# Four graph layers on one core: the opening reordered, idle TensorE slots filled, and the two arms of a branch exchanged

## The chip, the cores and the metric

The kernel runs on one core of a Trainium2 chip. The metric is the device time of the program in microseconds; three runs of the kernel before gave 1700.79, 1702.48 and 1705.91, median 1702.48. The core has a matrix engine (TensorE, PE in the profile, with its weight loads listed as PEld), a vector engine (VectorE, DVE), an activation engine (ScalarE, ACT), a general engine (GpSimd, POOL) and a queue engine (SyncE, SP) that issues every data transfer here. Each engine takes its own list of instructions in order and waits on semaphores where it needs another's result.

## The reference, cut to what matters

32 graphs of 512 nodes with 128 features share one adjacency matrix of 512 by 512 zeros and ones. Each of four layers adds its result for `relu(layernorm(x))` to `x`:

```
x = x + gnn0(h)      # x_h = elu(h @ Wi + bi); e = sigmoid(a_tgt[i] + a_src[j] + be) * mask[i, j]
                     # recv = elu([e @ x_h, x_h * sum_j e] @ Wn + bn); out = [recv, x_h] @ Wm + bm
x = x + gnn1(h)      # 5 steps of a gated unit on m = adj @ h:
                     #   z, r = sigmoid(...); hv = tanh(m @ w5 + (r * h) @ u5); h = (1 - z) h + z hv
x = x + gnn2(h)      # adj @ (h @ weight) + bias
x = x + gnn3(h)      # sum over powers 0 to 3 of adj, each with a weight
```

`mask` is `adj`, with 0.005 in place of its zeros.

## The kernel before

A graph is a 128 x 512 tile, and most operations work on one such tile: TensorE products in float32 against a 128 x 128 weight, copies and activations on ScalarE, additions on VectorE. Graphs are loaded in groups of four; the last layer works on a whole group.

**The order is written out beforehand.** The kernel lists operations with an engine, an assumed duration and a due time, and the class `Plan` sorts them into one order by list scheduling: at each moment of its own clock each engine takes the ready operation that is due first, provided that its buffers are free (36 of kind `f`, 8 PSUM banks of kind `b`, and so on). The order of the instructions of each engine is therefore fixed when the kernel is built; on the chip only semaphores move them. The due time of graph b starts at `begin(b)` (L627): 10 planner microseconds per graph for the first ones (`FIRST_PACE`), 56 per graph in the steady part, 30 at the end.

**Two arms.** Products with the adjacency can take a cheap path with a rounded float32 format (`float32r`), in which one operand is split into a high and a low part, if the adjacency is exactly representable in it. The kernel tests this on the chip: the adjacency is transposed on TensorE (L464), copied as `A_r` in the rounded format by ScalarE (L466), compared with the original on VectorE (L472, with a count per partition), and TensorE sums the counts (L479) into `inexact` (L484). The operations whose planned start lies before `BRANCH`, 30 planner microseconds, are issued first; then every engine loads `inexact` (L906) and branches (L907). Behind it stand two complete orders of all the rest, `arm(False)` for any adjacency, written first, and `arm(True)` for an exact one, written second and reached by a jump. The adjacency of this case is exact.

**What precedes the branch.** SP issues the loads in the order graph 0, `Wi`, the four adjacency blocks `A_nat`, `bi`, the token weights `W_tok`, `be`, graph 1, `Wn` and the others, graphs 2 and 3. Each graph's `layernorm` (L425) takes statistics on DVE (L434 to L437), an inverse square root on POOL (L439) and scaling on ACT (L447). `layer0` (L503) transposes h on TensorE (L334), copies it (L394), multiplies by `Wi` (L405), applies `elu` (three activations L492, L410, L495, two DVE steps L497, L499), multiplies into tokens and scores (L521), spreads the target scores (L558), forms four masked score tiles (L572 on ACT, L575 on DVE), aggregates with four products (L583), sums rows with four products against `ones` (L590 through L405), and continues with `Wn` (L611) and `Wm` (L619). `mask` comes from two steps for each transposed block (L468, L469).

**After the branch** the arm transposes the gate weights (L674), permutes the adjacency (L757), and runs layers 1 to 3. Layer 1's step has the adjacency product (L769), three gate weights, and the candidate product with `u5T`, which waits for DVE's reset gate times h (L801). Layer 3 is L850 and L859.

Of the kernel before, what the change touches and what calls it, by code (L numbers as in the profile page):

```python
# [10 lines left out]
F32 = mybir.dt.float32  # L11
# [3 lines left out]
ALU = mybir.AluOpType  # L15

P = 128
ALPHA = 0.005
# [20 lines left out]
class Plan:  # L39
# [13 lines left out]
    def op(self, eng, us, due, emit, reads=(), writes=(), two=False, keep=0, result=None):  # L53

        o = Op(eng, us, self.RESULT[eng] if result is None else result, emit, two, keep)
        for v in reads:
            o.before.add(v.writer)  # L60
        for v in writes:
            o.before.update(v.readers)
            if v.writer:
                o.before.add(v.writer)
            elif v.kind and v.slot is None:
                o.takes.append(v)
        for v in reads:
            v.readers.append(o)
# [34 lines left out]
    def order(self, end=None):  # L103
# [82 lines left out]
def tile_four_graph_layers(  # L186
# [79 lines left out]
    ident, ones, neg_half = const("ident", [P, P]), const("ones", [P, P]), const("nhalf", [P, NC])  # L266
    op("POOL", 1.0, -9, lambda: make_identity(nc, at(ident)), [], [ident])
    op("DVE", 0.2, -9, lambda: nc.vector.memset(at(ones), 1.0), [], [ones])
    op("POOL", 0.2, -9, lambda: nc.gpsimd.memset(at(neg_half), -0.5), [], [neg_half])
    ones_r = const("ones_r", [P, P], F32R)  # L270
    op("POOL", 0.4, 5, lambda: nc.gpsimd.tensor_copy(at(ones_r), at(ones)), [ones], [ones_r])
# [3 lines left out]
        at(warm)[:, :1], at(ones)[:, :1], AF.Tanh), [ones], [warm])  # L275


    def load(v, src, due, us=0.5, to=None):
        op("SP", us, due, lambda: nc.sync.dma_start(at(v) if to is None else to(at(v)), src), [], [v])
        return v  # L280

    def load_const(src, shape, name, due, us=0.5):
        return load(const(name, shape), src, due, us)
# [8 lines left out]
    plan.vals.update(dict.fromkeys([*X_group, *X]))  # L292

    def load_graph(b, due):
        op("SP", 1.5, due, lambda: nc.sync.dma_start(
            at(X[b]), x[b].rearrange("(c p) d -> p c d", p=P)),
            [], [X_group[b // G], X[b]] if b % G == 0 else [X[b]])

    load_graph(0, -9)
    Wi_sb = load_const(Wi, [P, P], "Wi_sb", -9)  # L300
    A_nat = [Val("f") for _ in range(NC)]
    for ic in range(NC):
        load(A_nat[ic], adj[ts(ic, P), :], -8, 1.3)
    bi_sb = load_column(bi, "bi_sb", -8)
# [6 lines left out]
    load_graph(1, -6)  # L311
# [145 lines left out]
    A_r, mask = const("A_r", [P, NC, N], F32R), const("mask", [P, NC, N])  # L457
    inexact = const("inexact", [1, 1], I32)
    n_odd = const("n_odd", [P, NC])
    for jc in range(NC):  # L460
        pt, z, odd = Val("b"), Val("f"), Val("f")
        def turn(jc=jc, pt=pt):
            for ic in range(NC):
                nc.tensor.transpose(at(pt)[:, ts(ic, P)], at(A_nat[ic])[:, ts(jc, P)], at(ident))  # L464
# [3 lines left out]
        op("ACT", T_COPY, jc, lambda z=z, pt=pt: nc.scalar.mul(at(z), at(pt), 1 / ALPHA), [pt], [z])  # L468
        op("DVE", T_VEC, jc, lambda jc=jc, z=z, pt=pt: nc.vector.scalar_tensor_tensor(  # L469
            at(mask)[:, jc, :], at(pt), 0.0, at(z), op0=ALU.is_equal, op1=ALU.add),  # L470
            [pt, z], [mask])
# [173 lines left out]
    issue(plan.order(end=BRANCH))  # L645
    assert inexact.writer.begun
    common = plan.state()

    def arm(exact):
        with ExitStack() as stack:  # L650
            pool = stack.enter_context(tc.tile_pool(name=f"arm{exact:d}", bufs=1))
            plan.back_to(common)
            list_rest(exact, pool)
            issue(plan.order())

# [251 lines left out]
    with tc.If(taken > 0) as branch:  # L907
        arm(False)
    with branch.Else():
        arm(True)  # L910


# [33 lines left out]
```

## Time and profile before

| | |
|---|---|
| Three runs, median | 1702.48 us (1700.79 to 1705.91) |
| The profiled execution's own time | 1704.23 us |
| Its span | 1702.4 us |
| Busy in the span: PE, DVE, ACT, POOL | 1665.6, 1478.8, 1099.6, 377.3 us |
| Mean granted TensorE clock | 0.996 |
| Data moved | 156.5 MB, 92 GB/s |

The page gives busy time per engine, the same in 40 equal slices (a digit is the busy share in tenths, PEclk the granted clock in tenths), the chain of work that ended last, and groups of instructions. A line of a timeline reads: start and duration in us, engine, source line, operation, result and operands, number of records, and in brackets the idle time before it with what ended it. A float32 product appears as two records. In answers by stretch, the columns are the stretch, its length and then busy time with the number of instructions for each engine, the granted clock, the share of the transfer engines and GB/s. The names of an engine with a q at the end are its sequencer.

### The profile page before, as it was taken

To read this page: it belongs to the slowest core of one execution; us is meant where nothing else is said; L and a number is where in the kernel's file an instruction comes from. 1 tells how busy PE (TensorE), PEld (TensorE's weight loads), DVE (VectorE), ACT (ScalarE), POOL (GpSimd) and SP (SyncE) were. 2 spreads that over 40 slices of the span, in tenths; PEclk is the share of its full clock that TensorE was granted. 3 is DMA by queue.
4 is the path that set the end of the run, shared out by engine and by line. 5 is a ranking of instruction groups with operands and counts; after the bars stand their busy time and mean duration, and the time that the engine had idled before them with its cause. 6 is when DMAs were issued, how large, how long until landed. Compare 5 with 4: busy or idle time off the path is not lost.

```text
span 1702.4 us, 21136 instructions
## 1 busy us (share of the span) xinstructions
PE 1665.6 (98%) x6521; PEld 1065.7 (63%) x6521; DVE 1478.8 (87%) x3325; ACT 1099.6 (65%) x2075; POOL 377.3 (22%) x301
## 2 busy tenths in 40 slices
PE   5999999999999999999999999999999999999998
PEld 3565555666666666665666665666666666666787
DVE  5789999999989998889989898899999888877842
ACT  5786767777666776566676666667576756655550
POOL 3231122312312222222212222122232221001210
PEclk8999999999999999999999999999999999999999
DMA  3122323253333332242333333333333323222302
GB/s 95 36 69 93 123 96 99 70 150 92 93 99 112 100 105 88 76 123 93 94 108 91 94 107 87 100 107 107 89 112 95 95 86 101 81 75 75 95 6 62
DMA packets 266873, 156.54 MB, mean 92 GB/s; under 512 B 75392, under 2 KB 235008, under 8 KB 266752
## 3 DMA queue, kind: packets, MB, share of 16 engines
q1 hardware_dynamic: 266752, 155.12, 30.9%
q8 instruction: 53, 0.87, 0.2%
q14 instruction: 68, 0.56, 0.1%
HBM read 82.25 MB, written 72.81 MB: 91 GB/s over the span
## 4 chain that ended last, share of the span: by engine, by line
PE 84%; DVE 8%; DMA 3%; ACT 3%; issue 2%; SPq 0%; POOL 0%; DVEq 0%; ACTq 0%; POOLq 0%
PE b L405 39%; PE b L769 18%; PE b L859 9%; PE b L850 6%; PE b L583 4%; PE b L619 3%; DMA f<-d 2%; PE b L521 2%; DVE f L575 2%; PE b L833 1%; DVE r L743 1%; PE b L606 1%; ACT f L447 1%; DVE f L794 1%; DVE f L346 1%
## 5 line engine op out<-in xcount | busy, mean ns | idle before, releaser
L394 ACT COPY f<-b 128x512 f32<-128x512 f32 x360 | 207.8, 585 | 151.6 <-PE b L769 105.8
L769 PE MATMUL b<-AQ,r 128*128 128x512 f32 x1024 | 304.4, 439 | 0.8 <-DVE r L743 0.8
L439 POOL TENSOR_TENSOR s<-s,nhalf 128x4 f32<-128x4 f32 x128 | 156.0, 1219 | 645.8 <-DVE s L437 610.1
L769 PEld LDWEIGHTS b<-AQ,r 128*128 128x128 f32 x1024 | 192.1, 188 | 90.5 <-issue 49.9
L794 DVE TENSOR_TENSOR f<-f,b 128x512 f32<-128x512 f32 x320 | 211.8, 677 | 20.4 <-PE b L405 16.5
L447 ACT ACTIVATE f<-x,s 128x128 f32<-128x128 f32 x512 | 210.1, 488 | 23.0 <-DVE s L442 22.7
L346 DVE STREAM_TRANSPOSE f<-f 128x512 f32<-128x512 f32 x244 | 204.6, 845 | 22.3 <-ACT f L447 21.7
L859 PE MATMUL b<-r,A_r 128*128 128x512 f32 x768 | 223.6, 426 | 0.0
L410 ACT ACTIVATE f<-f,b4w 128x512 f32<-128x512 f32 x160 | 115.4, 723 | 165.2 <-DVE f L794 164.7
L594 POOL TENSOR_TENSOR f<-f,f 128x512 f32<-128x512 f32 x84 | 130.9, 1559 | 307.3 <-DVE f L575 231.0
L405 PE MATMUL b<-f,u5T 128*128 128x512 f32 x320 | 163.9, 596 | 7.9 <-DVE f L801 7.8
L859 PEld LDWEIGHTS b<-r,A_r 128*128 128x128 f32 x768 | 139.0, 189 | 44.9 <-issue 23.0
L405 PE MATMUL b<-f,w4T 128*128 128x512 f32 x320 | 163.4, 593 | 0.2 <-ACT f L394 0.2
L405 PE MATMUL b<-f,u3T 128*128 128x512 f32 x320 | 163.0, 592 | 0.4 <-DMA f<-m 0.4
L405 PE MATMUL b<-f,w5T 128*128 128x512 f32 x320 | 162.8, 592 | 0.0
L405 PE MATMUL b<-f,w3T 128*128 128x512 f32 x320 | 162.5, 592 | 0.0
L769 PE MATMUL b<-A_r,r 128*128 128x512 f32 x512 | 151.8, 439 | 2.5 <-DVE r L743 2.5
L410 ACT ACTIVATE f<-b,b5w 128x512 f32<-128x512 f32 x160 | 109.2, 684 | 64.5 <-PE b L405 63.5
L743 DVE TENSOR_TENSOR r<-f,r 128x512 fp32r<-128x512 f32 x192 | 143.1, 749 | 8.2 <-ACT r L739 8.1
L850 PEld LDWEIGHTS b<-V,f 128*128 128x128 f32 x1024 | 130.5, 192 | 24.8 <-issue 20.6
L410 ACT ACTIVATE f<-f,b3w 128x512 f32<-128x512 f32 x160 | 115.2, 720 | 42.5 <-DVE f L794 41.6
L811 DVE TENSOR_TENSOR f<-f,f 128x512 f32<-128x512 f32 x160 | 114.7, 718 | 29.3 <-ACT f L410 28.7
(103 smaller groups left out, 2623.8 us busy)
## 6 DMA issues: line engine op xcount, KB each, us to landing
m<-f SPq DMA_DIRECT2D x244, 256.0 KB, 2.1
f<-m SPq DMA_DIRECT2D x184, 256.0 KB, 2.9
f<-m SPq DMA_DIRECT2D x240, 64.0 KB, 2.2
x<-in_x_dram SPq DMA_DIRECT2D x32, 256.0 KB, 3.1
out_dram<-x SPq DMA_DIRECT2D x32, 256.0 KB, 2.4
f<-d SPq DMA_DIRECT2D x28, 256.0 KB, 5.1
f<-in_adj_dram SPq DMA_DIRECT2D x4, 256.0 KB, 4.0
f<-in_L_gnn_weight_dram SPq DMA_DIRECT2D x2, 224.0 KB, 3.3
```

The lines of the kernel that those rows point to most:

```text
L346: op("DVE", us, due, lambda: nc.vector.transpose(view_out(at(blocks)), view_in(at(src))), [src], [blocks])
L394: op("ACT", us, due, lambda: nc.scalar.copy(at(t), at(src)), [src], [t])
L405: nc.tensor.matmul(to, at(w), of, start=start, stop=stop)
L410: op("ACT", us, due, lambda: nc.scalar.activation(at(dst), at(src), AF.Tanh, bias=at(bias), scale=scale), [src, bias], [dst])
L439: op("POOL", 1.2, due, lambda: nc.gpsimd.tensor_tensor(stat(SCALE), stat(VAR), at(neg_half), op=ALU.pow), [s, neg_half], [s])
L447: nc.scalar.activation(at(h)[:, ts(c, P)], at(X[b])[:, c, :], AF.Relu, bias=stat(SHIFT)[:, c : c + 1], scale=stat(SCALE)[:, c : c + 1],)
L594: op("POOL", 1.4, d - 10, lambda: nc.gpsimd.tensor_tensor(at(dst), at(a), at(c), op=ALU.add), [a, c], [dst])
L743: op("DVE", T_VEC, due, lambda: nc.vector.tensor_tensor(part(lo), whole(), part(hi).bitcast(F32), op=ALU.subtract), [src, hi], [lo], two=two)
L769: nc.tensor.matmul(at(pa), at(part)[:, ts(jc, P)], view(at(columns)[:, jc, :]), start=jc == n == 0, stop=jc == NC - 1 and n == PARTS - 1,)
L794: op("DVE", T_VEC, d, lambda: nc.vector.tensor_tensor(at(s), at(u), at(pg), op=ALU.add), [u, pg], [s])
L850: nc.tensor.matmul(at(pz)[:, ts(i, D)], at(hT[i])[:, ts(ic, P)], at(V[k]), start=i == 0, stop=last and i == G - 1,)
L859: nc.tensor.matmul(at(pz), at(adjT)[:, jc, ts(ic, P)], at(part), start=False, stop=jc == NC - 1 and n == PARTS - 1,)
```

## The change

- **Loads.** Graph 1 is loaded right behind graph 0, `bi` ahead of the adjacency, graph 2 right behind it, graph 3 ahead of `Wm`; `bm_bc` may not start before the branch.
- **Exactness test.** The test no longer uses the transposed blocks: ACT copies each natural block to a rounded tile `short`, and DVE compares it with the block. The transposes become due at 8, the masks at 9 to 12, and the `A_r` copies at 22.
- **Idle TensorE.** Up to the branch, whenever the planner finds no operation for TensorE, it puts in a 128 x 128 product of `ones` with `ones` into one PSUM bank that is set aside for this and given back at the branch. In the resulting order there are 31 of them at the head, then 1, 1, 15, 1 and 3 between other operations.
- **Planner.** Up to the branch, an engine now leaves a slot empty if an earlier-due operation becomes ready within 0.3 of the duration of the one at hand. Graph loads count 0.65 instead of 1.5, adjacency loads 0.65 instead of 1.3; `FIRST_PACE` is 14 instead of 10; `BRANCH` is 18 instead of 30, so that the branch stands earlier in the list of operations.
- **Arms.** The condition is turned round: `arm(True)` is written first and follows the branch directly; `arm(False)` is reached by the jump. The end of each arm goes to the common end behind both.

```diff
     def op(self, eng, us, due, emit, reads=(), writes=(), two=False, keep=0, result=None,
+           earliest=0.0):
...
+        o.earliest = earliest
...
-            o.ready = max([0.0, *(self.known(b, o) for b in o.before if b.begun)])
+            o.ready = max([o.earliest, *(self.known(b, o) for b in o.before if b.begun)])
...
+                if o is not None and end is not None and any(
+                    c.due < o.due and t < now + 0.3 * o.us for t, _, c in coming[e]
+                ):
+                    heapq.heappush(ready[e], (o.due, index[o], o))
+                    o = None
+                if o is None and e == "PE" and end is not None and self.idle.known <= now:
+                    order.append(self.idle)
+                    self.until[e] = now + self.idle.us
+                    heapq.heappush(events, self.until[e])
...
-    PACE, FIRST_PACE, LAST_PACE = 56.0, 10.0, 30.0
-    BRANCH = 30.0
+    PACE, FIRST_PACE, LAST_PACE = 56.0, 14.0, 30.0
+    BRANCH = 18.0
...
+    spare = places["b"].pop()
+    plan.free["b"].pop()
+    plan.idle = Op("PE", 0.224, 0.0, lambda: nc.tensor.matmul(
+        spare[:, :P], at(ones), at(ones), start=True, stop=True), False, 0)
+    plan.idle.known = 0.4
...
     load_graph(0, -9)
+    load_graph(1, -9)
     Wi_sb = load_const(Wi, [P, P], "Wi_sb", -9)
+    bi_sb = load_column(bi, "bi_sb", -9)
...
-    bm_bc = load_const(bm.partition_broadcast(P), [P, P], "bm_bc", -5)
-    load_graph(2, -4)
-    load_graph(3, -3)
+    bm_bc = load_const(bm.partition_broadcast(P), [P, P], "bm_bc", -5, earliest=BRANCH)
+    load_graph(3, -6)
...
+    for ic in range(NC):
+        short, odd = Val("q"), Val("f")
+        op("ACT", T_COPY, 9, lambda ic=ic, short=short: nc.scalar.copy(
+            at(short), at(A_nat[ic])), [A_nat[ic]], [short])
+        op("DVE", 0.7, 9, lambda ic=ic, short=short, odd=odd: nc.vector.scalar_tensor_tensor(
+            at(odd), at(short).bitcast(F32), 1.0, at(A_nat[ic]),
+            op0=ALU.mult, op1=ALU.not_equal, accum_out=at(n_odd)[:, ic : ic + 1]),
+            [short, A_nat[ic]], [odd, n_odd], two=True)
...
-        op("PE", T_TR, jc, turn, [*A_nat, ident], [pt])
-        op("ACT", T_COPY, jc, lambda jc=jc, pt=pt: nc.scalar.copy(at(A_r)[:, jc, :], at(pt)),
+        op("PE", T_TR, 8, turn, [*A_nat, ident], [pt])
+        op("ACT", T_COPY, 22, lambda jc=jc, pt=pt: nc.scalar.copy(at(A_r)[:, jc, :], at(pt)),
...
-        op("DVE", 0.7, 8, lambda jc=jc, pt=pt, odd=odd: nc.vector.scalar_tensor_tensor(
-            at(odd), at(A_r)[:, jc, :].bitcast(F32), 1.0, at(pt),
-            op0=ALU.mult, op1=ALU.not_equal, accum_out=at(n_odd)[:, jc : jc + 1]),
-            [A_r, pt], [odd, n_odd])
...
-    with tc.If(taken > 0) as branch:
+    with tc.If(taken < 1) as branch:
+        arm(True)
+    with branch.Else():
         arm(False)
-    with branch.Else():
-        arm(True)
```

More of the change, by code (lines that the diff above doesn't have):

```diff
@@ L51, in __init__, with op @@
         self.shared, self.now = 0.0, 0.0
-    def op(self, eng, us, due, emit, reads=(), writes=(), two=False, keep=0, result=None):
+        self.idle = None
+    def op(self, eng, us, due, emit, reads=(), writes=(), two=False, keep=0, result=None,
+           earliest=0.0):
         o = Op(eng, us, self.RESULT[eng] if result is None else result, emit, two, keep)
+        o.earliest = earliest
         for v in reads:
@@ L275, in tile_four_graph_layers, with load, load_const @@
         at(warm)[:, :1], at(ones)[:, :1], AF.Tanh), [ones], [warm])
-    def load(v, src, due, us=0.5, to=None):
-        op("SP", us, due, lambda: nc.sync.dma_start(at(v) if to is None else to(at(v)), src), [], [v])
-        return v
-    def load_const(src, shape, name, due, us=0.5):
-        return load(const(name, shape), src, due, us)
+    def load(v, src, due, us=0.5, to=None, earliest=0.0):
+        op("SP", us, due, lambda: nc.sync.dma_start(at(v) if to is None else to(at(v)), src), [], [v],
+           earliest=earliest)
+        return v
+    def load_const(src, shape, name, due, us=0.5, earliest=0.0):
+        return load(const(name, shape), src, due, us, earliest=earliest)
     def load_column(src, name, due):
@@ L294, in load_graph @@
     def load_graph(b, due):
-        op("SP", 1.5, due, lambda: nc.sync.dma_start(
+        op("SP", 0.65, due, lambda: nc.sync.dma_start(
             at(X[b]), x[b].rearrange("(c p) d -> p c d", p=P)),
@@ L299, in tile_four_graph_layers @@
     load_graph(0, -9)
+    load_graph(1, -9)
     Wi_sb = load_const(Wi, [P, P], "Wi_sb", -9)
+    bi_sb = load_column(bi, "bi_sb", -9)
     A_nat = [Val("f") for _ in range(NC)]
     for ic in range(NC):
-        load(A_nat[ic], adj[ts(ic, P), :], -8, 1.3)
-    bi_sb = load_column(bi, "bi_sb", -8)
+        load(A_nat[ic], adj[ts(ic, P), :], -8, 0.65)
+    load_graph(2, -8)
     W_tok = const("W_tok", [P, P + 2])
@@ L310, in tile_four_graph_layers @@
     be_sb = load_const(be.partition_broadcast(P), [P, 1], "be_sb", -7)
-    load_graph(1, -6)
     Wn_sb = load_const(Wn[P:], [P, P], "Wn_sb", -6)
@@ L459, in tile_four_graph_layers @@
     n_odd = const("n_odd", [P, NC])
+    for ic in range(NC):
[6 more added lines that the diff above has]
+            [short, A_nat[ic]], [odd, n_odd], two=True)
     for jc in range(NC):
-        pt, z, odd = Val("b"), Val("f"), Val("f")
+        pt, z = Val("b"), Val("f")
         def turn(jc=jc, pt=pt):
@@ L464, in turn @@
                 nc.tensor.transpose(at(pt)[:, ts(ic, P)], at(A_nat[ic])[:, ts(jc, P)], at(ident))
-        op("PE", T_TR, jc, turn, [*A_nat, ident], [pt])
-        op("ACT", T_COPY, jc, lambda jc=jc, pt=pt: nc.scalar.copy(at(A_r)[:, jc, :], at(pt)),
+        op("PE", T_TR, 8, turn, [*A_nat, ident], [pt])
+        op("ACT", T_COPY, 22, lambda jc=jc, pt=pt: nc.scalar.copy(at(A_r)[:, jc, :], at(pt)),
            [pt], [A_r])
-        op("ACT", T_COPY, jc, lambda z=z, pt=pt: nc.scalar.mul(at(z), at(pt), 1 / ALPHA), [pt], [z])
-        op("DVE", T_VEC, jc, lambda jc=jc, z=z, pt=pt: nc.vector.scalar_tensor_tensor(
+        op("ACT", T_COPY, 9 + jc, lambda z=z, pt=pt: nc.scalar.mul(at(z), at(pt), 1 / ALPHA), [pt], [z])
+        op("DVE", T_VEC, 9 + jc, lambda jc=jc, z=z, pt=pt: nc.vector.scalar_tensor_tensor(
             at(mask)[:, jc, :], at(pt), 0.0, at(z), op0=ALU.is_equal, op1=ALU.add),
             [pt, z], [mask])
-        op("DVE", 0.7, 8, lambda jc=jc, pt=pt, odd=odd: nc.vector.scalar_tensor_tensor(
-            at(odd), at(A_r)[:, jc, :].bitcast(F32), 1.0, at(pt),
-            op0=ALU.mult, op1=ALU.not_equal, accum_out=at(n_odd)[:, jc : jc + 1]),
-            [A_r, pt], [odd, n_odd])
     p_odd = Val("b")
@@ L647, in tile_four_graph_layers @@
     common = plan.state()
+    places["b"].append(spare)
     def arm(exact):
@@ L652, in arm @@
             plan.back_to(common)
+            plan.free["b"].append((BRANCH, len(places["b"]) - 1))
             list_rest(exact, pool)
```

## The prediction

> **What bounds the kernel now.** I read the page's busy shares and 40 slices first, then busy time by stretch, then TensorE's timeline over the first 45 us, then the chain and the branch line.
>
> ```profile
> span 1702.4 us, 21136 instructions
> PE 1665.6 (98%) x6521; PEld 1065.7 (63%) x6521; DVE 1478.8 (87%) x3325; ACT 1099.6 (65%) x2075; POOL 377.3 (22%) x301
> PE   5999999999999999999999999999999999999998
> PEclk8999999999999999999999999999999999999999
> ```
>
> TensorE is the bound from the second slice on. It is idle 1702.4 - 1665.6 = 36.8 us in all; only there, and where its clock is halved, can a rearrangement gain. The stretches say where (span, PE, PEld, DVE, ACT, POOL, then the clock):
>
> ```profile
> 0.00:10.00 10.00, 3.11 (x12) 2.50 (x13) 1.65 (x11) 4.31 (x9) 2.49 (x12) 1.00 0.69 194
> 10.00:20.00 10.00, 3.14 (x12) 2.06 (x10) 8.71 (x39) 5.47 (x10) 3.82 (x4) 0.80 0.19 55
> 20.00:30.00 10.00, 8.25 (x29) 5.08 (x30) 4.95 (x13) 7.63 (x18) 3.60 (x3) 0.52 0.16 47
> 30.00:40.00 10.00, 7.84 (x28) 4.03 (x27) 3.70 (x15) 5.33 (x12) 2.42 (x4) 1.00 0.43 108
> 40.00:50.00 10.00, 8.95 (x38) 5.25 (x37) 8.46 (x27) 8.99 (x22) 3.99 (x7) 1.00 0.00 0
> 200.00:400.00 200.00, 198.44 (x669) 114.81 (x668) 193.58 (x424) 142.19 (x269) 51.02 (x37) 1.00 0.35 104
> ```
>
> 18.7 us of the idle time lie before 50; from 50 to 200 there is none, from 200 to 1500 some 13.2, after the last matmul 5. DVE at 97% in 200 to 400 is the second bound. TensorE's head:
>
> ```profile
> 6.89 1.63 PE L334 MATMUL b<-ident,f 128*128 128x128 f32 x4 [6.89 <-ACT f L447]
> 8.31 3.62 PE L464 MATMUL b<-ident,f 128*128 128x128 f32 x16
> 11.73 1.42 PE L405 MATMUL b<-f,Wi_sb 128*128 128x512 f32 x2
> 20.61 2.10 PE L521 MATMUL b<-W_tok,f 128*128 128x130 f32 x8 [7.46 <-DVE f L499]
> 26.33 2.08 PE L405 MATMUL b<-f,Wi_sb 128*128 128x512 f32 x2 [1.14 <-ACT f L394]
> 28.20 3.43 PE L583 MATMUL b<-f,f 128*128 128x512 f32 x6
> 31.46 0.60 PE L334 MATMUL b<-ident,f 128*128 128x128 f32 x4
> 34.22 1.12 PE L583 MATMUL b<-f,f 128*128 128x512 f32 x2 [2.16 <-DVE f L499]
> ```
>
> Full-clock prices are in later rows: four transposes 0.44, a 128x512 float32 product 0.86, a token product 0.9 for four, a 128x128 product 0.2225 (1.78 for eight of L619). At these prices the work done before 34.22 is 20 transposes 2.2, Wi twice 1.72, tokens 0.9, count 0.3, spread 0.44, a second and a third graph's transposes 0.88, three of L583 2.58: 9.0 us. So 25.2 us are lost by 34.22, and 1.05 more by 46.2: 26.3. The pieces: 6.9 before the first, 3.2 to 13.15 (slow or paced), 7.5 waiting for graph 0's elu, 2.5 slow, 1.1 idle, 1.7 slow, 2.3 at the branch. The branch's own line, and DVE's idle time behind it:
>
> ```profile
> L907 PEldq COMPARE_BRANCH  x1: 4549/4549/4549, 29.6 to 29.6; - x1
> 32.39 0.69 DVE L497 SCALAR_TENSOR_TENSOR f<-f,f 128x512 f32<-128x512 f32 x1 [4.03 <-issue]
> ```
>
> [...]clock 0.50 from 16 to 29.6, L521 2.10 us there and 1.06 later; the 1.00 shown before 10 does not hold, since sixteen transposes take 3.62 us against 1.76. [...]4.55 us on PE, whose exact arm is the jump's target. [...]the other engines' own records are 45 to 76 ns[...].
>
> **The change part by part.** I walk the new order of each engine with the durations above.
>
> *Loads.* Graph 1 goes ahead of Wi and the adjacency: one 256 KB load, 0.65 us as the adjacency blocks land one after another; plus bi, the four blocks land at about 8.4 instead of 7.5. Hidden, as the fillers end later. Graph 3 passes Wm and the score weights on SP's queue; the score weights, last before the branch, are issued when the last block lands and are there 3.5 later, at 11.9, ahead of the tokens at 17.45. bm_bc moves behind the branch (issued 20.5, landing in 3.9), so POOL's bias additions start near 24.5 instead of 14.8; behind them on POOL wait only gate biases, swap and later norms, and DVE's first addition to x comes after 40. Costs nothing.
>
> *Fillers.* 52 products of ones: 31 from 1.05, then 1, 1, 15, 1, 3 as slots of the fixed order. At 0.445 each while cold; [...]they end at 9.7 to 11.4. I take 10.55. Were they unneeded, transposes could start at 8.4: they cost 2.1 here and buy the clock everywhere after. They take one PSUM bank, given back at the branch; the order found places with seven.
>
> *Graph 0.* Eight adjacency transposes, a filler, h's four: 12.1. ACT copies hT to 12.9, PE does eight more and a filler to 13.2 and Wi to 14.1. ACT's three masks end at 14.65, exp, tanh and relu at 16.55, DVE's second elu step at 17.25; 15 fillers end at 17.45: tokens 17.45 to 18.35, against 20.61 to 22.7.
>
> *Exactness test.* It reads the natural blocks, so four more ACT copies (2.3 us; ACT is 65% busy) while PE runs fillers, and DVE's tests no longer wait for A_r. The count comes at 18.4, inexact at 19.5 instead of 23.5. Two of the A_r copies slip past the branch, ahead of their use at L783 by 8 us.
>
> *Graph 1.* Norm on ACT to 18.8, transposes 19.2, three fillers, spread 20.0 to 20.45, Wi 20.7 to 21.6 (before: 26.33 to 28.2).
>
> *Branch.* The exact arm falls through: a tensor load of 0.5 and a compare of 0.05 in each sequencer, under ACT's score and PE's Wi. Graph 0's first aggregation (28.20 above, in the old order) begins at 22.6: four aggregations 3.44, four row sums 3.44, 0.9 lost waiting for graph 2's norm on ACT, tokens of graph 1, five weight transposes, spread, graph 2's Wi, Wn, four permuting products: 12.3 us of work end at 35.5. Work before the branch is 6.0, so 35.5 - 18.3 = 17.2 us are lost where 26.3 were. After that my walk finds no wait. Gain 9.1.
>
> *The end.* The exact arm now ends with a jump over the other arm. PE's sequencer is at the end at 1693.3 and DVE's at 1697.55, so theirs is hidden. SP issues its last store to 1698.92 and then steps through waits that end at 1701.57, for the store's landing at 1701.45. At SP's 2.7 us from the compare to its first step in the arm it arrives at 1701.6 and needs 0.5 more: +0.7 with the barrier. [...]+2.4 at PE's 4.5. I take 0.7.
>
> *The middle.* Line and wait stay the same:
>
> ```profile
> PE b L405 <- DVE f L801: 7.8, 7, 1.9
> ```
>
> A candidate product (u5) waits for DVE's reset times h. By counts from the new order and the row prices, PE's own work between a w4 product and its u5 product is under 4 us in 16 of 160 places, 23 before. DVE work queued ahead of the 48th adjacency product is about 388 us instead of 394. So no worse; I take 0, with -4 to +5.
>
> Sum: -9.1 + 0.7 + 0 = -8.4: the profiled span goes from 1702.4 to 1694.0 and its own time from 1704.2 to 1695.8. The median of the runs, 1702.5, equals the span, so the forecast is 1694.1.
>
> **The rivals.** *Slower: DVE takes over.* Layers 0 of graphs 4 and 5 are put 16 and 14 planner microseconds later (first pace 14 for 10), toward the stretch where DVE has only 6.4 us spare in 200. One such layer is about 9.8 us of DVE (norm 1.4, four masks 2.5, two elus 2.6, the rest single steps of 0.65 to 0.85), two 19.6. If all of it leaves the 19 us that DVE has free between 50 and 200, PE waits 19.6 - 6.4 = 13 us near 300 to 450: 1707. It decides from 8.4 us. For it: the 97%, and 5.2 us of PE idle between 350 and 500 already. Against: the smaller DVE queue ahead of the 48th product.
>
> *Fillers stay cold.* If none of the 31 is at full clock they end at 14.9, and all after is 4.3 later: 1698.4. For it: TensorE stayed at 0.50 through 4.6 busy us from 20.61.[...]
>
> *The branch doesn't get cheaper.* If falling through costs PE's 4.55 too, the first aggregation is at about 25.7, 3.1 later: 1697.2.[...]
>
> *DVE hides part of the gain* without turning it: 3 to 5 us of new waits, 1697 to 1699.
>
> **How the numbers follow.** Forecast 0.60, with its own range 1690 to 1698; cold fillers 0.07, dear branch 0.06, DVE hiding part 0.11, DVE taking over 0.16. About 0.3% (5.1 us) is what a measurement of this kernel can tell from no change: faster means under 1697.4, slower over 1707.6. The forecast case gives 0.55 faster and 0.05 same; the three middle cases 0.07 and 0.17; the last 0.02 same and 0.14 slower, being centred at 1707 but open upward. Faster 0.62, same 0.24, slower 0.14. The lower end 1689 takes in a middle that loses 4 less; the upper 1704 the middle cases and a part of the last.
>
> **What would show it.** Right: clock 1.00 from about 6 on with no dip, inexact near 19.5, PE's branch record near 0.05, the first aggregation near 22.6, PE idle plus fillers about 17 by 35. SP's last wait some 0.7 us later after its last store. Wrong: PE idle from 200 to 1500 well over 13 us with L801's or L743's successors as its releasers, a second elu step later than 17.5, or fillers that end after 11.5.

## The result, and the profile after

The changed kernel took 1713.45 us (median of 6 runs, 1710.08 to 1715.30) against 1703.74 for the kernel before (6 runs in the same comparison): ratio 1.0056, 95% interval 1.0042 to 1.0070. It is about 10 us slower. The forecast was 1694.1, with a range up to 1704, so the result lies outside it and on the other side.

The page of the changed kernel, in the rows that answer to those of before:

```profile
span 1713.5 us, 21323 instructions
PE 1679.7 (98%) x6625; PEld 1076.3 (63%) x6625; DVE 1480.9 (86%) x3325; ACT 1100.2 (64%) x2079; POOL 379.9 (22%) x301
PE   9999999999999999999999999999999999999998
PEclk9999999999999999999999999999999999999999
```

The first slice is full now, and yet the span is 11.1 us longer. Fillers count as busy here (15.1 us), so a busy share does not show the loss. By stretch (span, PE, PEld, DVE, ACT, POOL, clock, share of the transfer engines, GB/s):

```profile
10.00:20.00 10.00, 10.00 (x91) 9.37 (x90) 7.90 (x29) 8.39 (x19) 1.84 (x3) 1.00 0.09 22
20.00:30.00 10.00, 7.21 (x28) 3.57 (x26) 8.33 (x24) 9.12 (x20) 7.17 (x11) 0.99 0.55 146
30.00:40.00 10.00, 10.00 (x34) 5.88 (x34) 5.26 (x18) 6.38 (x14) 3.04 (x3) 0.84 0.02 6
200.00:400.00 200.00, 195.25 (x672) 113.03 (x671) 195.47 (x421) 142.19 (x268) 49.06 (x35) 1.00 0.36 104
```

TensorE's timeline at the head, changed kernel:

```profile
1.04 9.46 PE L285 MATMUL b<-ones 128*128 128x128 f32 x62 [1.04 <-DVE ones L280]
17.17 1.06 PE L545 MATMUL b<-W_tok,f 128*128 128x130 f32 x8
21.96 2.84 PE L607 MATMUL b<-f,f 128*128 128x512 f32 x6 [0.64 <-DVE f L599]
29.25 0.33 PE L700 MATMUL b<-ident,f 128*128 128x128 f32 x1 [2.15 <-DVE f L698]
31.07 2.91 PE L425 MATMUL b<-f,ones 128*128 128x512 f32 x4
```

Graph 0's tokens start at 17.17 (forecast 17.45), its first aggregation (L607, before L583) at 21.96 (forecast 22.6). Up to there the head came out as walked. The waits between 50 and 1650 did not. TensorE's waits (us in total, times, longest), first two rows of before that stand beside the one shown in the prediction (L801, 7.8 us in 7), then those of the changed kernel (L405, L583, L801, L743 of before are L425, L607, L827, L769 now):

```profile
PE b L769 <- DVE r L743: 3.3, 2, 2.5
PE b L583 <- DVE f L575: 1.0, 1, 1.0
```

```profile
PE b L607 <- DVE f L599: 8.1, 9, 1.8
PE b L425 <- DVE f L827: 8.0, 7, 1.9
PE b L630 <- DVE q L625: 3.0, 4, 1.2
PE b L795 <- DVE r L769: 2.0, 2, 1.2
```

The candidate products wait as before. New are the aggregations of later graphs behind their masked scores (L607), and the row sums (L630): 12.7 us in 12 waits became 22.5 in 26.

**A ledger of lost time.** To compare whole executions I price every TensorE record at full clock from this kernel's own rows: 0.4292 us for a float32 record with 512 columns, 0.2267 for one in float32r, 0.1115 for 128 columns, 0.1095 for a transpose, 0.03 for a record of the count, 0 for a filler. The sum is 1639.1 us in every kernel below. At any moment, the time minus the price of what has begun is what TensorE has lost: waits, slow clock, and small gaps between records. I split it into head (up to 50 us), middle (from 50 to the end of the last product) and end (from there to the end of the span):

```
kernel                                head  middle   end    sum = span - 1639.1
before                                27.1    31.3   4.9    63.3
changed                               20.1    47.5   6.8    74.4
changed, a second execution           20.6    51.9   7.0    79.5
```

The head gained 7.0, the end lost 1.9, and the middle lost 16 to 21 us, which the prediction had put at 0. Each row of this ledger, here and below, is one execution. Executions of the kernel before alone lie between 1700.17 and 1712.14 us, so a difference of a few us between two rows counts only where the ratios below agree with it.

### The profile page after: what moved, and what is told of

Its sections match the earlier page's. It is cut to its first block, busy times and chain, and to the rows that moved or that the text cites. A ratio compares the mean times of both kernels' runs of the same rounds, so it can differ in the third digit from the quotient of the medians.

```text
span 1713.5 us, 21323 instructions
## 1 busy us (share of the span) xinstructions
PE 1679.7 (98%) x6625; PEld 1076.3 (63%) x6625; DVE 1480.9 (86%) x3325; ACT 1100.2 (64%) x2079; POOL 379.9 (22%) x301
## 4 chain that ended last, share of the span: by engine, by line
PE 76%; DVE 14%; DMA 4%; ACT 3%; issue 2%; SPq 0%; DVEq 0%; ACTq 0%
PE b L425 34%; PE b L795 16%; PE b L885 9%; PE b L876 6%; PE b L607 3%; DMA f<-d 3%; PE b L643 3%; DVE f L599 2%; DVE f L366 2%; DVE r L769 1%; PE b L545 1%; DVE f L820 1%; PE b L859 1%; DVE f L841 1%; DVE f L839 1%
## 5 line engine op out<-in xcount | busy, mean ns | idle before, releaser
L795 PE MATMUL b<-AQ,r 128*128 128x512 f32 x1024 | 303.9, 439 | 1.2 <-DVE r L769 0.8
L795 PEld LDWEIGHTS b<-AQ,r 128*128 128x128 f32 x1024 | 192.2, 188 | 92.1 <-issue 48.4
L425 PE MATMUL b<-f,u5T 128*128 128x512 f32 x320 | 164.0, 597 | 8.0 <-DVE f L827 8.0
L885 PEld LDWEIGHTS b<-r,A_r 128*128 128x128 f32 x768 | 139.2, 189 | 47.3 <-issue 25.4
L425 PE MATMUL b<-f,w4T 128*128 128x512 f32 x320 | 163.5, 594 | 0.0
L425 PE MATMUL b<-f,u3T 128*128 128x512 f32 x320 | 162.7, 592 | 0.0
L425 PE MATMUL b<-f,w5T 128*128 128x512 f32 x320 | 162.3, 592 | 0.0
L425 PE MATMUL b<-f,w3T 128*128 128x512 f32 x320 | 161.9, 592 | 0.0
L769 DVE TENSOR_TENSOR r<-f,r 128x512 fp32r<-128x512 f32 x192 | 140.6, 737 | 12.3 <-ACT r L765 12.0
L795 PE MATMUL b<-A_r,r 128*128 128x512 f32 x512 | 150.0, 435 | 1.2 <-DVE r L769 1.2
L430 ACT ACTIVATE f<-f,b3w 128x512 f32<-128x512 f32 x160 | 115.0, 720 | 47.5 <-DVE f L820 45.6
L837 DVE TENSOR_TENSOR f<-f,f 128x512 f32<-128x512 f32 x160 | 108.8, 681 | 29.2 <-ACT f L430 28.8
```

What stands on the lines that cost most here:

```text
L425: nc.tensor.matmul(to, at(w), of, start=start, stop=stop)
L430: op("ACT", us, due, lambda: nc.scalar.activation(at(dst), at(src), AF.Tanh, bias=at(bias), scale=scale), [src, bias], [dst])
L769: op("DVE", T_VEC, due, lambda: nc.vector.tensor_tensor(part(lo), whole(), part(hi).bitcast(F32), op=ALU.subtract), [src, hi], [lo], two=two)
L795: nc.tensor.matmul(at(pa), at(part)[:, ts(jc, P)], view(at(columns)[:, jc, :]), start=jc == n == 0, stop=jc == NC - 1 and n == PARTS - 1,)
L885: nc.tensor.matmul(at(pz), at(adjT)[:, jc, ts(ic, P)], at(part), start=False, stop=jc == NC - 1 and n == PARTS - 1,)
```

## Experiments

The prediction was a gain at the head that reaches the end. Two explanations stood against each other after the result. **Order** (theory A in the expectations): the planner writes the whole rest of the program anew, and the new order is worse. **Taken back** (theory B): TensorE is coupled to DVE, ACT and transfers, so whatever is gained at the head is waited away later. Ratios are to the kernel before in the same comparison, with 95% intervals.

### One part of the change at a time

The kernel before with only the arms exchanged, and the changed kernel with the arms in their old places. Beyond the branch the instructions of each engine stand in the same order as without the edit.

```diff
-    with tc.If(taken > 0) as branch:
-        arm(False)
+    with tc.If(taken < 1) as branch:
+        arm(True)
     with branch.Else():
-        arm(True)
+        arm(False)
```

> The kernel before with nothing changed but the condition and the places of the two arms; every engine's order of instructions in the exact arm stays as it was. Theory A (the re-planned order of the middle is what costs, whatever the head delivers): the head gains [...]some 2 to 3 us by 50 us, the middle keeps its lost time of 31 us between 50 and 1690, the end pays some 1.9 us as in the changed kernel: within 1 us of before. Theory B (DVE and the transfers are a second bound and any head gain is given back in the middle): the middle's lost time grows by the 2 to 3 us: 1.5 to 2.5 us slower than before.

> The changed kernel with the arms in their old places, the exact one reached by the jump; all else, orders included, stays. Theory A: lost time at 50 us grows from 20.1 by 2 to 4, the middle keeps 47, the end gets the 1.9 us back: the changed kernel's time, plus 0 to 2 us. Theory B: the later start is absorbed in the middle, and only the end's 1.9 us show: some 2 us faster than the changed kernel.

Exchanged in the kernel before: 1705.22 us, ratio 0.9999 (0.9988 to 1.0010); head 25.4, middle 31.3, end 6.9. Falling through gains 1.7 at the head, the end pays 2.0, and the middle is 31.3 in both, as theory A had it. So a gain at the head can reach the last product. Put back in the changed kernel: 1708.28, ratio 1.0023 (1.0012 to 1.0034); head 21.0, end 4.9, but a middle of 38.3 instead of 47.5, with the same order of instructions. These two rows exaggerate: the 38.3 is of the fastest of ten executions (1705.14), the 47.5 of the slowest of six (1715.30). By the ratios the kernel with the arms put back is some 5.6 us faster (1.0023 against 1.0056), and neither theory had forecast that.

The end is a jump of SP. Rows of the common end in the changed kernel (operation, count, ns, first and last start):

```profile
L933 SPq COMPARE_BRANCH  x2: 46/48/49, 20.1 to 1708.7; - x2
L933 PEldq COMPARE_BRANCH  x2: 92/1691/3290, 20.6 to 1702.4; - x2
```

```profile
L967 SPq DRAIN  x3: 7/7/13, 1712.7 to 1713.0; - x3
```

SP compares at 1708.7, right behind its last store, and is in its closing drain 4.0 us later; in the trace its first step behind the jump is at 1712.18, 3.4 us after the compare. In the kernel before, SP gets from its last store (issued by 1698.92) to that drain (1701.57) in 2.65 us, the wait for the store's landing included. PE's jump takes 3.29 us too, at 1702.4, but PE's last product ends only at 1706.7.

The changed kernel without fillers (the slots stay in the plan and emit nothing), and with 32 more of them ahead of everything:

```diff
-    plan.idle = Op("PE", 0.224, 0.0, lambda: nc.tensor.matmul(
-        spare[:, :P], at(ones), at(ones), start=True, stop=True), False, 0)
+    plan.idle = Op("PE", 0.224, 0.0, lambda: None, False, 0)
```

```diff
-    issue(plan.order(end=BRANCH))
+    early = plan.order(end=BRANCH)
+    first = early.index(plan.idle)
+    issue(early[:first] + 32 * [plan.idle] + early[first:])
```

> The changed kernel without its 52 products of ones; the planner still reserves their slots, so that every other instruction keeps its place. Shows what the fillers are worth. Theory A: TensorE is at half clock for most of the head, lost time at 50 us rises from 20 to 22 to 26, the middle keeps 47: 2 to 6 us slower than the changed kernel. Theory B: the middle takes up the delay: within 1 us of the changed kernel.

> The changed kernel with 32 more products of ones ahead of its 31, which delays all TensorE work by 32 x 0.2225 = 7.1 us and undoes the head's gain; no other order changes. Theory A: the middle keeps its lost time of 47 us and the whole is 6 to 7 us slower than the changed kernel, near 1720. Theory B: the middle's lost time falls to about 40 and the time stays within 2 us of the changed kernel.

Without: 1709.15, ratio 1.0024 (1.0015 to 1.0033), head 21.0, middle 42.1. With more: 1715.34, ratio 1.0061 (1.0041 to 1.0080), head 24.7, middle 43.0. The fillers are worth only 1 us at the head, and the kernel without them is faster, which neither theory had forecast. A head that is 4.6 us later costs nothing that shows against the changed kernel (1.0061 against 1.0056), as theory B had it. One order of the middle, four heads: 38 to 52 us, and 47.5 and 51.9 with one and the same head. The order alone does not fix the loss, nor does the head.

### The pace, and one transfer that the planner takes for too short

The changed kernel with the old pace of the first graphs, the kernel before with the new one, and the changed kernel once more beside them:

```diff
-    PACE, FIRST_PACE, LAST_PACE = 56.0, 14.0, 30.0
+    PACE, FIRST_PACE, LAST_PACE = 56.0, 10.0, 30.0
```

> The changed kernel with the first pace back at 10 instead of 14. Theory C (the room that the order leaves on TensorE between a graph's token products and its first aggregation sets the middle's loss; it is under 11 us for 6 of the 24 graphs 4 to 27 in the changed kernel, for 2 in the kernel before and for 2 here): the middle loses 33 to 38 us instead of 47, and the time is 1700 to 1706. Theory D (the pace has nothing to do with it, any re-plan behind this head costs as much): 1709 to 1715.

> The kernel before with the first pace at 14 and nothing else. Room under 11 us for 3 graphs of 24. Theory C: the middle loses 31 to 35 us, within 4 us of before. If the first pace itself is to blame: the middle loses 40 or more, 1710 or slower.

> The changed kernel once more, beside the others of this call. Its ratio to the kernel before was 1.0056; the three kernels with the same middle order and another head stood at 1.0023, 1.0024 and 1.0061. If the head doesn't matter for the middle (theory A), this one lies near 1.004 to 1.006, since it has the best head; if it lies at 1.0025, the earlier figure was a spread of the runs.

The changed kernel again: 1717.39, ratio 1.0063 (1.0050 to 1.0076). With pace 10 it is 1708.80, ratio 1.0014 (1.0007 to 1.0021), middle 41.0. The kernel before with pace 14: 1715.78, ratio 1.0058 (1.0045 to 1.0071), middle 44.2. One constant moves 9 us, in either direction. For a moment the pace looked like the cause. The theory of the room ahead of the aggregations (C) missed both: it had 1700 to 1706 for the first and, for the second, no more than 4 us beyond before. Its rival D, with 1709 to 1715 for the first, was just missed too.

The waits of L607 go back to the broadcast read of the target scores (L572 of the changed kernel, 256 KB out of rows of 512 bytes). The chain of the changed kernel that ends in the longest of them (`m<-f` is another transfer, for which SP waits 3.7 us before it can issue the read):

```profile
996.29 4.46 DMA m<-f
...
1001.28 5.12 DMA f<-d
1006.41 0.02 issue
1006.43 0.73 ACT f L596
1007.16 0.02 issue
1007.19 3.60 DVE f L599 x4
```

The planner has 3.6 us for this read; its median landing is 5.1 us before and 5.4 after. Told 6.0:

```diff
-            op("SP", T_DMA, d, read, [row], [tgt], keep=KEEP, result=3.6)
+            op("SP", T_DMA, d, read, [row], [tgt], keep=KEEP, result=6.0)
```

> The changed kernel with one number of the planner changed: the read of the scores' row from DRAM, broadcast to 128 partitions, counts 6.0 until its data are there instead of 3.6 (in the traces it lands 5.1 to 5.4 us after its issue). The order then leaves at least 13.2 us between tokens and first aggregation for every graph 4 to 27. Theory C: TensorE's waits for the aggregations (8.1 us in 9 places) vanish and the row sums' too (3.0), the middle loses 30 to 36 us, the time is 1697 to 1704 and below the kernel before or equal. Theory D: it stays within 3 us of the changed kernel.

1711.03, ratio 1.0026 (1.0016 to 1.0035), middle 42.4. The aimed-at waits are gone, and others have grown:

```profile
PE b L425 <- DVE f L827: 10.3, 10, 1.8
PE b L795 <- DVE r L769: 8.0, 4, 3.0
PE b L607 <- DVE f L599: 0.5, 1, 0.5
```

That the aimed-at waits went fits the read as their cause, but only 6.4 us of the changed kernel's time beside it came back: theory C had 1697 to 1704 us, D at most 3 us, and neither came. Each of these edits also writes a new order, so none says by itself what the edit did.

### Orders drawn at random

So I changed constants that have nothing to do with the work: a pace between the two, an ACT copy taken for 0.51 instead of 0.50, a transfer's issue for 0.46 instead of 0.45, each in the kernel before.

```diff
-    PACE, FIRST_PACE, LAST_PACE = 56.0, 10.0, 30.0
+    PACE, FIRST_PACE, LAST_PACE = 56.0, 12.0, 30.0
```

```diff
-    T_VEC, T_COPY, T_ACT, T_DMA = 0.61, 0.5, 0.6, 0.45
+    T_VEC, T_COPY, T_ACT, T_DMA = 0.61, 0.51, 0.6, 0.45
```

```diff
-    T_VEC, T_COPY, T_ACT, T_DMA = 0.61, 0.5, 0.6, 0.45
+    T_VEC, T_COPY, T_ACT, T_DMA = 0.61, 0.5, 0.6, 0.46
```

> The kernel before with the first graphs 12 planner microseconds apart, between its own 10 and the change's 14. Theory 'pace' (the wider the first graphs stand apart, the more the middle loses, because their work moves toward a stretch with no room): half of what 14 cost, ratio about 1.003 (1.002 to 1.004), lost time from 50 to 1690 about 37. Rival 'draw' (the planner writes another order for all 1650 us behind the head, and the order of before happens to be one of the better ones): no trend is owed; anything from 1.001 to 1.008, as likely above the 14's 1.0058 as below it. By the new order 3 graphs have under 11 us of TensorE work between token products and first aggregation (before 2, after 6), and 16 places under 4 us between a w4 and its u5 product (before 23, after 16).

> The kernel before with one assumed duration of the planner a hair longer (an ACT copy 0.51 instead of 0.50); paces, loads, arms and work as before. Theory 'pace': nothing that matters is changed, so within 2 us of before, ratio 0.999 to 1.001. Rival 'draw': a new order is a new draw, 3 to 12 us slower, ratio 1.002 to 1.007, with the loss between 50 and 1690 rather than at the head, lost time there 34 to 43 instead of 31.

> The kernel before with another assumed duration of the planner a hair longer (a transfer's issue 0.46 instead of 0.45). A second draw: theory 'pace' wants 0.999 to 1.001 again; rival 'draw' wants 1.002 to 1.007, and a value unlike that of the ACT copy's.

```
before with                ratio (95%)               head  middle   end
pace 12                    1.0121 (1.0102..1.0141)   27.9    47.8   5.0
ACT copy 0.51              1.0011 (1.0000..1.0022)   26.2    34.5   4.9
transfer's issue 0.46      1.0042 (1.0026..1.0058)   26.7    43.7   4.9
pace 14 (from above)       1.0058 (1.0045..1.0071)   24.5    44.2   4.9
```

Pace 12 costs more than twice what 14 does, beyond even the range of the 'draw' theory: there is no trend. A hundredth of a microsecond in an assumed issue time costs 0.4%, as that theory had it. In the copy's duration it costs 0.1%, between the two forecasts. These heads differ from before's by at most 2.6 us; the middle differs by 3 to 17. Before's 31.3 is the best of all the orders seen here. Pace 12 shows the kinds of wait that the changed kernel shows, and that before has less of:

```profile
PE b L405 <- DVE f L801: 10.3, 11, 1.9
PE b L583 <- DVE f L575: 5.8, 7, 1.4
PE b L405 <- ACT f L394: 2.7, 3, 1.5
```

The counter-test keeps before's order and improves only the head, with fillers ahead of the first transpose and of graph 0's tokens:

```diff
-    issue(plan.order(end=BRANCH))
+    fill = Op("PE", 0.0, 0.0, lambda: nc.tensor.matmul(
+        places["b"][7][:, :P], at(ones), at(ones), start=True, stop=True), False, 0)
+    early = plan.order(end=BRANCH)
+    on_pe = [o for o in early if o.eng == "PE"]
+    for n, o in ((12, on_pe[0]), (24, on_pe[6])):
+        i = early.index(o)
+        early[i:i] = n * [fill]
+    issue(early)
```

> The kernel before, its planned order kept instruction for instruction, with 36 products of ones put into TensorE's list ahead of the branch: 12 ahead of its first transpose, 24 ahead of graph 0's tokens. If the order of the middle decides what the middle loses, this keeps before's: lost time from 50 to 1690 stays at 31 (29 to 33). The clock should stay released through the tokens, the spread and graph 1's Wi (slow from 16 to 29.6 before), which frees about 3 us at the head: lost at 50 some 24 instead of 27.1, time 1703 or less where before has 1706, ratio 0.998 (0.9970 to 0.9995). If instead whatever the head gains is taken back later, the middle shows 33 to 35 and the ratio is 1.000.

1706.35, ratio 1.0000 (0.9989 to 1.0012); head 24.9, middle 34.6. Of the 3 us expected at the head 2.2 came, and the middle lost them again: a gain of 2.2 (0.9987) lies just outside the interval. That was the taken-back rival's forecast.

### Crossing head and order

All runs so far change an order and a head together, or the head alone. The last three cross them. Up to the branch each is one kernel, instruction for instruction; behind it stands everything that is left in the order of the other, written out as a list of operations with their planned ends, with buffers taken along that list:

```diff
+ORDER = [
+...
+]
...
+    def replay(self, base):
+        left = [o for o in self.ops if not o.begun]
+        listed = {i - base: o for i, o in enumerate(self.ops) if i >= base and not o.begun}
+...
+        for o, known in todo:
+            o.begun = True
+            for v in o.takes:
+                v.slot = self.free[v.kind].pop(0)[1]
+...
-            issue(plan.order())
+            issue(plan.replay(BASE) if exact else plan.order())
```

> The changed kernel up to the branch, instruction for instruction, and behind it everything that is left in the order of the kernel before (written out as a list; buffers are taken in that order too), arms as in the change. Theory 'the new order of the middle is what costs': the middle keeps before's loss (lost from 50 to 1690 about 31, at most 35), the head keeps the change's gain (lost at 50 about 20), the exchanged arms cost 1.9 at the end: 1700 to 1703 where before has 1706, ratio 0.9965 to 0.9985. Rival 'the head's gain is taken back whatever stands behind it': ratio 1.000 to 1.002, middle loss 37 to 39. Rival 'the new head itself disturbs the middle': ratio 1.004 or more, middle loss over 41.

> The reverse: the kernel before up to its branch, and behind it what is left in the order of the changed kernel; arms as before. Theory 'new order costs': the middle loses 41 to 50 from 50 to 1690, lost at 50 about 27; ratio 1.006 to 1.010 (before's 1706 plus 10 to 17). Rival 'head disturbs the middle': no slower than before, 0.999 to 1.002. Rival 'taken back': about the changed kernel's own 1.006, or less, with a middle loss of about 40.

> The first of these three with the arms in their old places (exact arm last, reached by the jump). The end is 1.9 shorter, the branch at the head dearer by about 1.7 to 3 on TensorE. By what the exchange alone did to the kernel before (ratio 0.9999) the time should be within 1.5 us of the first's; ratio 0.9960 to 0.9985 under 'new order costs', and this or the first should then be the fastest of all kernels here.

```
head      order behind it   arms   us        ratio (95%)               head  middle   end
before    before            old    1705.61   1                         27.1    31.3   4.9
changed   before            new    1703.63   0.9988 (0.9975..1.0001)   19.5    35.6   6.9
changed   before            old    1704.44   0.9993 (0.9980..1.0005)   23.2    34.0   4.9
before    changed           old    1713.48   1.0040 (1.0023..1.0057)   24.6    44.3   4.9
changed   changed           new    1713.45   1.0056 (1.0042..1.0070)   20.1    47.5   6.8
```

(The last row is from the first comparison, where before had 1703.74; the first four are of one comparison.) With the old order the changed head is no slower than before; with the new order before's own head is 7.9 us slower by the medians, 0.40% (6.8 us) by the ratio. That rules out a new head that disturbs the middle by itself. The middles came near what the order theory had (35.6 for at most 35, 44.3 for 41 to 50), but all three ratios lie outside its ranges, on the side of a smaller effect. The waits between 50 and 1650 follow the order, not the head. Changed head with old order, where L1475, L1658, L1846 are L405, L583, L769 of before:

```profile
PE b L1475 <- DVE f L1878: 8.0, 6, 2.1
PE b L1658 <- DVE f L1650: 3.9, 6, 1.9
PE b L1846 <- DVE r L1820: 3.3, 2, 2.5
```

and before's head with the new order, where L1633, L1454, L1656, L1819 are L607, L425, L630, L795 of the changed kernel:

```profile
PE b L1633 <- DVE f L1625: 7.8, 10, 1.7
PE b L1454 <- DVE f L1851: 7.0, 6, 1.9
PE b L1656 <- DVE q L1651: 3.0, 4, 1.2
PE b L1819 <- DVE r L1793: 2.0, 2, 1.2
```

The last two rows of the second fence equal the changed kernel's to the digit. (Before's own order replayed behind before's own head was not run; waits that come out this equal speak against a cost of the replay itself.) So the order is the main cause: 13.0 of the 16.2 us of middle in the first execution of the changed kernel (44.3 - 31.3), and 0.40 of its 0.56% by the ratios. What makes this order worse than the old one, beyond the waits in which it shows, stays open. And the taken-back rival is right for the rest: with the old order, 7.6 us gained at the head have shrunk to 3.3 at the last product, and the exchanged arms take 2.0 of these. The waits of the aggregations (L1658 above, 3.9 against 1.0) hold 2.9 of the 4.3 given back.

Head and order do not simply add: -2.0 and +7.9 make +5.9, and the whole change costs +9.7 and, in its second comparison, +10.6 (by the ratios, -0.12 and +0.40 make +0.28%, against 0.56 and 0.63). With the arms in their old places they do add within the intervals: -0.07 and +0.40, against +0.23% for the changed kernel with its arms put back. The difference can be seen in the waits that reach about 2 us, behind some of which the clock fell to 0.50 (behind 1.93 and 3.23 us below, not behind 1.82). The same place in two executions of the changed kernel, first the first:

```profile
1007.93 4.03 PE L607 MATMUL b<-f,f 128*128 128x512 f32 x8 [1.82 <-DVE f L599]
```

```profile
1010.47 6.64 PE L607 MATMUL b<-f,f 128*128 128x512 f32 x8 [3.23 <-DVE f L599]
```

Eight such records take 3.60 us without a wait (at 38.43 in the changed kernel). Behind 1.82 us of waiting they took 4.03, behind 3.23 they took 6.64, at a clock of 0.50 in the second execution's stretches:

```profile
1010.00:1015.00 5.00, 4.53 (x6) 1.95 (x7) 5.00 (x7) 2.45 (x5) 3.21 (x2) 0.50 0.00 0
```

Such half-clock stretches of 3.4 to 6.8 us lie in the middle of both executions of the changed kernel (about 856 in both, and 1010 in the second), and in none of before or of the three crossed kernels (1.00 in every stretch of 200 us from 200 to 1600); with the arms put back the clock is 1.00 at these places (from 850 to 860 and from 1005 to 1010). Nor are there any with pace 12 (1.00 in all stretches from 50 to 1700), which loses as much, so a bad order does not need them. Against before's head with the new order they make up the rest. A stretch of 3.41 us at half clock gives away 1.7, so the one of the first execution costs 1.7 and the three of the second 5.1; TensorE's waits from 50 to 1650 are 22.5 and 24.0 there instead of 21.2. Together that is 3.0 and 7.9 us, where the middles exceed 44.3 by 3.2 and 7.6.

In the profiles of both kernels all changes of the granted clock lie on one grid of 3.41 us: in the first execution of the changed kernel at 29.72, 33.13, 855.74, 859.16 and 1709.08 (from the second to the third are 241 steps of 3.413), in before at 15.92, 29.58 and 1702.11 (4 and 490 steps). The windows ahead of the falls in the middle were not idle. Whole windows of that grid in the first execution,

```profile
852.33:855.74 3.41, 1.48 (x5) 0.68 (x4) 3.38 (x12) 2.75 (x6) 1.02 (x1) 1.00 0.34 107
1005.93:1009.34 3.41, 1.59 (x5) 0.69 (x5) 2.15 (x4) 2.91 (x5) 0.71 (x1) 1.00 0.01 3
```

and in the second:

```profile
1006.18:1009.59 3.41, 1.06 (x4) 0.23 (x3) 0.68 (x1) 0.62 (x1) 0.00 (x0) 1.00 0.21 48
```

The clock fell behind 1.48 and 1.06 us of busy time in a window, and not behind 1.59. Nor did it fall behind before's longest wait, 2.51 us from 427.3 on, which lies across two windows and leaves 1.75 us busy in the first. (These are single windows, and I draw no limit from them.) So what a wait cost here went with its place in the grid as well as with its length: 1.93 us of waiting inside one window, up to 854.91, was followed by 3.41 us at half clock, 2.51 us across two windows by none. That a head which shifts everything behind it shifts that place too is my inference.

The changed kernel with the arms put back has the same instructions at these places, and from 840 to 1020 TensorE waits 2.4 us there instead of 6.4. Most of the difference between the two executions is waits (15.6 against 22.5 us from 50 to 1650), and why the scores come earlier there I did not settle.

## Why the prediction was wrong

**The middle failed.** The step is "By counts from the new order and the row prices, PE's own work between a w4 product and its u5 product is under 4 us in 16 of 160 places, 23 before ... So no worse; I take 0, with -4 to +5". It measured +16 and +21. Two things were wrong in it. It counted one kind of wait, the largest that the profile of before showed, and the new order made others: the aggregations behind L599 and the row sums behind L625, 11.1 us where L583 had 1.0. And such a count does not rank orders: pace 12 has 16 tight places like the changed kernel and loses 47.8, an ACT copy of 0.51 has 29 and loses 34.5, before has 23 and loses 31.3. For the bound of +5 the prediction gives no ground. The draws show what it should have been: five orders of before's family lost 31 to 48. Its sign of being wrong, TensorE idle from 200 to 1500 well over 13 us, came (21.1), but more than half of that idle time was ended by other lines than the two that it named (L801 and L743 of before, 8.8 us).

**The head was right, and too large by 2.** Its gain was 7.0 at 50 instead of 9.1. The tokens, the exactness flag (19.03 for 19.5), the branch (0.092 on PE for 0.05) and the first aggregation came as walked. When the clock would come free under the fillers, and that falling through would be cheap, were my estimates; the profile of before shows neither. "After that my walk finds no wait" failed: L700 waits 2.15 us for DVE's addition of two weights (L698), which stands behind a new graph's statistics (L454 to L457) and an elu step (L523), and the clock is at half rate from 29.7 for 3.4 us, about 1.7 more. Nor do the fillers buy "the clock everywhere after": without them the head loses 21.0 instead of 20.1, so most of the gain is from the other parts of the change.

**The end was too small.** 1.9 to 2.0 instead of 0.7, below the +2.4 given beside it. SP needs 3.4 us from its compare to its first step, not the 2.7 of its branch in the middle of the program, and its last store is issued 2.0 us after the last product instead of 1.4.

**The sum's form was too simple.** It carried the head's gain to the end undiminished. That held where only the arms were exchanged (1.7 of 1.7), and not with the fillers in before's order (2.2 gone) or the changed head (7.6 became 3.3). The rival "DVE hides part of the gain" had put 3 to 5 us of new waits on this; the old order shows 4.3 us, 2.9 of them in waits for DVE's masked scores.

**The rivals.** "DVE takes over" named the pace, the mechanism "layers 0 of graphs 4 and 5 ... toward the stretch where DVE has only 6.4 us spare" and 1707. Undoing the pace does give 8.6 us back, but pace 12 costs more than 14, and from 200 to 400 TensorE waits 4.6 us instead of 1.3: a fraction of the 16, in many places and not in one. "Fillers stay cold" and "the branch doesn't get cheaper" were wrong: clock 1.00 in the stretch from 10 on, and 0.092 us on PE.

## What to carry to other kernels

Where a planner writes one fixed order, any edit that it sees, even of an assumed duration by 0.01 us, is two edits: the one meant, and a new draw of everything behind it; price the draw from a few neutral re-plans (here 0.1 to 1.2%, and before's order was the best seen) before believing a gain of half a per cent, and test the meant edit with the rest of the order held fixed. Do not carry a gain at the head to the end undiminished: with the order held fixed, 3.3 of 7.6 us arrived here, and all 1.7 where only the arms changed. Count the end of a branch's first arm as well as its beginning, on the queue that finishes last (here SP, 3.4 us for its jump).

## What the runs showed of the hardware that was not expected

- A jump at the end of an arm cost SP 3.4 us and PE 3.29 us in the changed kernel, and 1.9 to 2.0 us of the time in each pair of kernels that differ only in the arms (end 6.8 or 6.9 instead of 4.9; in the tables above 6.8 to 7.0 where SP has to jump last, 4.9 or 5.0 elsewhere).
- Behind a wait of 1.93 us TensorE's clock was 0.50 for 3.41 us (855.74 to 859.16 in the first execution of the changed kernel), behind one of 3.23 us for 6.8 (0.96, 0.50 and 0.86 in the three stretches of 5 us from 1005 to 1020 in the second), and the eight records that follow the latter took 3.0 us longer (6.64 instead of 3.60). The clock fell behind windows of 3.41 us in which TensorE was busy for 1.06 and 1.48 us, and not behind 1.59 or 1.75.
- The 31 products of ones at the head took 9.3 us where full clock would need 6.9. Their records start 0.213 us apart up to 5.68 us and 0.112 apart from 5.86 on (7 records lie in the stretch from 3 to 4, 12 in that from 6 to 7), so the clock came free between the two, near the forecast's "about 6", although the stretches show 1.00 from the start; yet all the fillers together were worth only 1 us.
